# Softmax normalization moved ahead of a unit's last part, and a routing table's steps moved by one, in a fused decoder layer

## The chip, the cores and the metric

One Trainium2 chip, one of its NeuronCores. The metric is the device time of one execution in microseconds (us), as the median of several runs. The engines are named as the profile names them: PE (TensorE matmuls), PEld (TensorE weight loads), DVE (VectorE), ACT (ScalarE), POOL (GpSimd), SP (SyncE, which issues most of the DMAs). Each engine works through its own instructions in order; between engines there are semaphores.

## The reference, cut to what matters

One pre-norm decoder layer for 16 batches of 128 tokens with 256 channels, all in float32:

```python
x = x + attn(layernorm(x))          # 16 heads; keys and values are one shared latent of 72
x = x + birwkv(layernorm(x), ctx, ctx, w, u)   # two decaying scans over the tokens
x = x + moe(layernorm(x))           # 8 experts, top 2, hidden 512

# attn, for each head h
Wdkv = x @ latent_w + latent_b
q = x @ Wd_w[h] + Wd_b[h]
scores = q @ Wdkv.T / sqrt(d_head), masked causally
p = softmax(scores)                 # exp(s - max), then divided by its sum
y[h] = p @ Wdkv
out = concat(y) @ out_w + out_b
```

The expert part sends each token to two of eight experts. The kernel therefore makes lists of tokens for each expert and, from the counts, tables of "slots": one slot is 128 tokens of one expert.

## The kernel before

**Units and steps.** The attention is cut into units: one batch and 4 of its 16 heads, so 64 units (`NU`), 4 to a batch. A loop over steps `s` writes all instructions in a fixed order (`manual_schedule`: no scheduler reorders them). Step s holds the scores of unit s (L442, PE), their negated row maxima (`maxima`, L459, DVE), their exponentials with row sums (`exps`, L467, ACT, four activations), a mask for the unit after next (L454, ACT), then the query projections of the next group of two batches (`query_tile`, L404 on PE, evacuated by L410 on ACT), and, for unit s-2, the transposes of its probabilities (`turn_probs`, L486 on PE, L488 `aT` on ACT), their product with the values (`values`, L494 `py`) and its evacuation (L506, L509).

Between them lies the **normalization** of a unit: the reciprocal of the four sums (L479, DVE) and the product of the 128x512 exponentials with it, in place (L480, POOL). In the kernel before, unit s-1 is normalized near the start of step s, and its transposes follow in step s+1.

**The plan.** All other work is put into a step by a table: `at(step, place, fn, ...)`, with the places "pre", "A", "B", "C" and "D" in the order in which `run(s, place)` is called in a step. "C" is the last part of a step in the attention stage; there is little in "D" before step 64. What lies in "C" and uses DVE or POOL:

- `wkv_exps` of batch b in step 4b+1: ACT exponentials (L533, L535), then two POOL products (L536, L537). The scan L545 on DVE in the next step reads L536's output.
- for a group of batches that begins at step z (8, 16, ... 48): `group_stats` in step z-3 (L305, L306 on DVE, L300 on POOL), `group_norm` in step z-2 (L320 on DVE, then ACT), `group_latents_out` in step z (L374 `kvT` on DVE, which frees a PSUM bank that the logits `pl`, L652, then use).
- parts of `route`, the choice of experts: for batches 0 to 3 in steps 25 to 27, for 4 to 7 in 41 to 43, for 8 to 11 in 57 to 59. The second part (L684 to L689, steps 25, 41 and 57) and the fifth (L726 to L737, steps 27, 43 and 59) lie in "C". They are small DVE instructions. Part four begins with the matmuls `pf` (L705 to L708) in step 27, 43 and 59, in a PSUM bank that a query projection used before.
- the parts of `first_table(0)`, which after 8 batches fixes the first 9 slots: six parts in six steps. Part 1 is a matmul `pc` (L758) in a PSUM bank of the query projections and five small DVE instructions (L760 to L770), part 2 is L830 to L834, part 3 is L776 to L784, part 4 is L792 and L794, part 5 is L801 to L807, part 6 is L809 to L815. Then `list_slots` (step 52, "C") reads the finished table into a register of SP (L842) and loads the first lists.

Two batches' tail stages share DVE and POOL with this: in step 4b+8 `residual` (L573, then L305, L306, L298, L300), in 4b+9 `mix_1` and `mix_2` (L602, L607, L608, then L609 on POOL), in 4b+10 `mix_stats`, in 4b+11 `mix_shift` (L320) and `mix_row` (L625, ACT), then the turn of the row for the logits (L640, L645) and the logits.

**After the attention.** From step 64 on each step takes one expert slot (`fetch`, `bring`, `turn`, `up`, `down`, L912 to L1026). This stage does not touch the lines of the change, but the last unit's normalization lies in step 64, behind `turn(0)`.

**PSUM.** The tag "t" has two banks, shared by all transposes (`pt`, `pxn`, `px`, `pw`, `pn`); "mm" has two, shared by `pq`, `pk`, `pl`, `pf` and `pc`.

```python
def normalize(b, hg):
    pr, sums = probs[b, hg], sums_of.pop((b, hg))
    rsum = small.tile([P, HG], F32, tag="rsum", name=f"rsum_{b}_{hg}")
    nc.vector.reciprocal(rsum, sums)
    nc.gpsimd.tensor_mul(pr, pr, rsum.unsqueeze(2).to_broadcast([P, HG, T]))
```

Of the kernel before, what the change touches and what calls it, by code (L numbers as in the profile page):

```python
# [22 lines left out]
C = 256  # L23
# [10 lines left out]
NHG = H // HG  # L34
NU = B * NHG
# [44 lines left out]
def decoder_kernel(  # L80
# [328 lines left out]
    def query_tile_out(g, i, pq, to):  # L409
        nc.scalar.activation(to, pq[:, :GT], AF.Identity, bias=bq_sb[:, i : i + 1], scale=0.25)  # L410
# [23 lines left out]
    def scores(b, hg):  # L434
        g, i = divmod(b, GB)
        n = b * NHG + hg
        ps = sbank(n)
        if n < 2:

            nc.tensor.matmul(ps, identb, maskb, start=True, stop=False)  # L440
        for j in range(HG):
            nc.tensor.matmul(  # L442
                ps[:, j, :],
                q[g, hg][0:L, j, ts(i, T)],
                kvT[g][:, ts(i, T)],
                start=False,
                stop=(j == HG - 1),
                skip_group_check=n >= 2,
            )
        pss[b, hg] = ps  # L450

    def lay_mask(n):

        nc.scalar.copy(sbank(n), maskb)  # L454

    def maxima(b, hg):
        ps = pss[b, hg]
        nm = small.tile([P, HG], F32, tag="nm", name=f"nm_{b}_{hg}")
        nc.vector.tensor_reduce(nm, ps, AX.X, ALU.max, negate=True)  # L459
        sums_of[b, hg] = nm  # L460
# [15 lines left out]
# [6 lines that stand above are left out]
    def turn_probs(b, hg):  # L482
        pt = bank("t", f"pt_{b}_{hg}").rearrange("p (j t) -> p j t", j=HG)
        pr = probs.pop((b, hg))
        for j in range(HG):
            nc.tensor.transpose(pt[:, j, :], pr[:, j, :], ident)  # L486
        aT = wk.tile([P, HG, T], F32, tag="aT", name=f"aT_{b}_{hg}")
        nc.scalar.copy(aT, pt)  # L488
        aTs[b, hg] = aT

    def values(b, hg):
        g, i = divmod(b, GB)
        py = bank("y", f"py_{b}_{hg}", bufs=1).rearrange("p (j t) -> p j t", j=HG)
        nc.tensor.matmul(  # L494
            py[:L], kvN[g][:, ts(i, L)], aTs.pop((b, hg)), start=True, stop=True
        )
        pys[b, hg] = py
# [426 lines left out]
    def bring(j):  # L924


        t, k = slots[j]
        to = []
        for n, (engine, copy) in enumerate(zip(experts, (nc.scalar.copy, nc.vector.tensor_copy))):
            into = experts[engine]  # L930
            if k % 4 == 0 or j in RARE:
                load_values(t, "ex", j, k, engine, E - 1, into)
            w = hpools[0].tile([P, WU0], F32, tag=f"w{n}", name=f"w{n}_{j}")
            copy(w, wall[:, bass.ds(into.pop(j), 1), n * WU0 : (n + 1) * WU0].rearrange("p o w -> p (o w)"))
            to.append(w)
        brought[j] = to

    def turn(j):
        xr = xrs.pop(j)
        pt = bank("t", f"pxr_{j}")  # L940
        for c in range(NC):
            nc.tensor.transpose(pt[:, ts(c, P)], xr[:, ts(c, P)], ident)  # L942
        xT = hpools[0].tile([P, NC, P], F32, tag="xT", name=f"xT_{j}")
        nc.vector.tensor_copy(xT, pt[:, : NC * P].rearrange("p (c t) -> p c t", c=NC))  # L944
        xTs[j] = xT
# [85 lines left out]
    def at(step, place, fn, *args):  # L1031
        plan.setdefault((step, place), []).append((fn, args))

    def run(step, place):
        for fn, args in plan.pop((step, place), []):
            fn(*args)
# [103 lines left out]
    for b in range(B):  # L1140
        s = NHG * b
        if b + 1 < B:
            at(s + 2, "pre", load_ctx, b + 1)
        at(s + 1, "C", wkv_exps, b)
        at(s + 2, "B", wkv_back, b)
        at(s + 3, "A", wkv_back_add, b)
        at(s + 4, "B", wkv_forth, b)
        at(s + 5, "A", wkv_forth_add, b)
        at(s + 5, "B", project, b, (0, 1))
        at(s + 6, "B", project, b, (2, 3))  # L1150
        at(s + 6, "C", rest_values, b)
        at(s + 7, "B", project, b, (4, 5))
        at(s + 7, "C" if b < B - 1 else "B", project, b, (6, 7, NP))
        for name, (step, place) in {B - 2: last_but_one, B - 1: last}.get(b, usual).items():
            at(s + step, place, stages[name], b)
        if b < E:
            for k in range(3):
                at(s + 11 + k, "C", load_expert, b, k)
        if b % RB == RB - 1:
            r = b // RB  # L1160
            parts = ((13, "B"), (13, "C"), (14, "B"), (15, "B"), (15, "C"))
            if b == B - 1:
                parts = ((12, "B"), (12, "D"), (13, "B"), (13, "D"), (14, "B"))
            for step, place in parts:
                at(s + step, place, route_part, r)
            for k in range(2 * RB):
                if b < B - 1:
                    at(s + 16 + k, "A", route_part, r)
                else:
                    at(s + 14 + (k + 1) // 3, "CDA"[(k + 2) % 3 if k > 1 else k], route_part, r)  # L1170
        if b + 1 in FIRST_B:
            i = FIRST_B.index(b + 1)
            parts = [(18 + k, "C") for k in range(6)]
            if i:
                parts = [(18, "C"), (20, "D"), (21, "B"), (21, "D"), (22, "D"), (23, "D")]
            for step, place in parts:
                at(s + step, place, table_part, i, first_table, i)
            for k in range(0, S1[i], 2):
                at(s + 24 + k // 2, "C", list_slots, min(2, S1[i] - k))
        if b == B - 1:  # L1180
            for k in range(7):
                at(s + 15 + k // 3, "ABD"[k % 3], table_part, "2", last_table)
            for k in range(0, S2, 4):
                at(s + 17 + k // 4, "C", list_slots, min(4, S2 - k))
            for k in range(4):
                at(s + 20 + k, "B", table_part, "3", very_last)
            for k in range(0, S3, 4):
                at(s + 24 + k // 4, "C", list_slots, min(4, S3 - k))
# [30 lines left out]
    def ahead(n, what):  # L1219
        if n < len(ORDER):  # L1220
            what(ORDER[n])
# [8 lines left out]
    for s in range(SLOT0 + len(ORDER) + 1):  # L1230
        j = s - SLOT0
        unit = divmod(s, NHG)
        past = divmod(s - 2, NHG)
        if s < NU:
            scores(*unit)
        if j == 0:

            st.close()
            hpools.append(ctx.enter_context(tc.tile_pool(name="hp", bufs=2)))
            turn(0)  # L1240
        if 1 <= s < NU + 1:
            normalize(*divmod(s - 1, NHG))
        run(s, "pre")
        if 2 <= s < NU + 2:
            turn_probs(*past)
        run(s, "A")
        if j == 0:
            bring(0)
        if s < NU:
            maxima(*unit)  # L1250
            exps(*unit)
            if s + 2 < NU:
                lay_mask(s + 2)
        g, i = divmod(s, UG)
        tiles = [(0, t) for t in late_tiles.get(s, [])]
        if g + 1 < NG:
            tiles += [(g + 1, t) for t in (TILES_1 if g == 0 else TILES)[i]]
        made = [(n, t, *query_tile(n, t)) for n, t in tiles[:2]]
        run(s, "B")
        if 2 <= s < NU + 2:  # L1260
            values(*past)
            values_out(*past)
        for n, t, pq, to in made:
            query_tile_out(n, t, pq, to)
        for n, t in tiles[2:]:
            query_tile_out(n, t, *query_tile(n, t))
        for n, t in tiles:
            if t == NP:
                rest_queries(n)
            if t == 5 and n:  # L1270
                odd_queries(n, 0)
            if t == 7:
                odd_queries(n, 1)
        if j >= 0:
            ahead(j + AHEAD, fetch)
            ahead(j + 1, bring)
            ahead(j, up)
        run(s, "C")
        if j >= 0:
            ahead(j + 1, turn)  # L1280
            if j >= 1:
                down(ORDER[j - 1])
        run(s, "D")
        if j == SF + S2 - SKIP:
            for r in RARE:
                if_used(r, whole_slot)
# [55 lines left out]
```

## Time and profile before

| | before |
|---|---|
| runs | 555.1, 555.19, 555.8 us; median 555.19 |
| profiled execution | 554.7 us, its span 553.0 us |
| granted PE clock, mean | 0.984 of full speed |
| PE busy, 25 to 320 us (attention) | 284.6 of 295 us |
| PE busy, 320 to 553 us (experts) | 211.5 of 233 us |
| ACT busy, 25 to 320 us | 251.4 us |
| DVE busy, 25 to 320 us | 217.6 us |
| POOL busy, 25 to 320 us | 198.8 us |

The profile is of one execution; the span runs from its first to its last instruction, and the time of the run is 1.7 us longer. In the timelines below a row is: start in us from the span's beginning, duration in us, engine, line of the kernel, operation, output<-inputs, shape, number of instructions, and in brackets the idle time of the engine just before it and who ended it. A wait for several semaphores is put down to the one that came last in the profile, which is not always the true one. The group rows of the page give busy us in all, mean ns of one, then the engine's idle us ahead of the group and what ended most of it.

### The profile page before, as it was taken

To read this page: it belongs to the slowest core of one execution; us is meant where nothing else is said; L and a number is where in the kernel's file an instruction comes from. 1 tells how busy PE (TensorE), PEld (TensorE's weight loads), DVE (VectorE), ACT (ScalarE), POOL (GpSimd) and SP (SyncE) were. 2 spreads that over 40 slices of the span, in tenths; PEclk is the share of its full clock that TensorE was granted. 3 is DMA by queue.
4 is the path that set the end of the run, shared out by engine and by line. 5 is a ranking of instruction groups with operands and counts; after the bars stand their busy time and mean duration, and the time that the engine had idled before them with its cause. 6 is when DMAs were issued, how large, how long until landed. Compare 5 with 4: busy or idle time off the path is not lost. (4 is left out here: it accounts for less than half of the span.)

```text
span 553.0 us, 10138 instructions
## 1 busy us (share of the span) xinstructions
PE 512.8 (93%) x3272; PEld 439.2 (79%) x3272; DVE 330.6 (60%) x831; ACT 329.3 (60%) x953; POOL 327.1 (59%) x379
## 2 busy tenths in 40 slices
PE   4889999999999999999998989999989999989990
PEld 3768787887777887877875679989979999989980
DVE  3354776687887678888769776555644533333330
ACT  1788998898797888888986873434313232313200
POOL 5356647564787774697646976454875454541532
PEclk9999999999999999999998999999989999999996
DMA  5432245364365545131121113232234232325321
GB/s 149 98 88 67 70 133 170 121 198 120 110 182 133 170 130 178 41 98 37 52 79 56 40 53 66 38 65 45 40 40 51 48 51 47 51 47 173 58 30 19
DMA packets 39662, 47.59 MB, mean 86 GB/s; under 512 B 14136, under 2 KB 31416, under 8 KB 39576
## 3 DMA queue, kind: packets, MB, share of 16 engines
q1 hardware_dynamic: 30106, 37.20, 23.0%
q0 software_dynamic: 7936, 9.51, 11.2%
q8 instruction: 28, 0.46, 0.3%
q10 hardware_dynamic: 1566, 0.21, 0.3%
q14 instruction: 26, 0.21, 0.2%
HBM read 28.22 MB, written 13.31 MB: 75 GB/s over the span
## 5 line engine op out<-in xcount | busy, mean ns | idle before, releaser
L467 ACT ACTIVATE pr<-s,nm 128x128 f32<-128x128 f32 x256 | 90.7, 370 | 9.7 <-DVE nm L459 9.5
L480 POOL TENSOR_TENSOR pr<-pr,rsum 128x512 f32<-128x512 f32 x64 | 75.7, 1183 | 33.5 <-DVE rsum L479 25.6
L990 ACT ACTIVATE sl<-s 128x512 f32<-128x512 f32 x36 | 21.5, 598 | 120.7 <-PE s L980 104.9
L1018 POOL DMA_INDIRECT acc<-y,en x28 | 47.5, 1697 | 60.4 <-DVE y L1013 29.8
L442 PEld LDWEIGHTS s<-kvT,q 72*128 72x128 f32 x512 | 65.7, 191 | 18.7 <-issue 12.6
L980 PEld LDWEIGHTS s<-xT,w 128*128 128x128 f32 x576 | 70.5, 195 | 9.4 <-issue 6.7
L980 PE MATMUL s<-xT,w 128*128 128x128 f32 x576 | 72.0, 279 | 5.4 <-DVE xT L944 2.3
L520 PE MATMUL po<-outw_sb,yP 128*128 128x256 f32 x288 | 74.4, 385 | 0.6 <-DMA yP<-yd 0.6
L442 PE MATMUL s<-kvT,q 72*128 72x128 f32 x512 | 70.5, 279 | 3.2 <-DMA q<-qr 2.2
L980 PE MATMUL pu<-xT,w 128*128 128x128 f32 x576 | 70.5, 276 | 0.0
L992 DVE TENSOR_TENSOR hT<-sl,pu 128x512 f32<-128x512 f32 x36 | 24.7, 687 | 74.1 <-PE pu L980 56.9
L1002 PE MATMUL pd<-wall,hT 128*128 x288 | 68.0, 379 | 0.0
L494 PE MATMUL py<-aT,kvN 128*72 128x512 f32 x128 | 66.4, 600 | 1.6 <-ACT aT L488 1.3
L980 PEld LDWEIGHTS pu<-xT,w 128*128 128x128 f32 x576 | 67.7, 193 | 0.0
L404 PE MATMUL pq<-xnT,wq_sb 128*128 128x256 f32 x256 | 65.3, 387 | 0.0
L520 PEld LDWEIGHTS po<-outw_sb,yP 128*128 128x128 f32 x288 | 54.0, 193 | 13.1 <-issue 5.2
L459 DVE TENSOR_REDUCE nm<-s 128x4 f32<-128x512 f32 x64 | 43.6, 682 | 30.5 <-PE s L442 30.5
L1002 PEld LDWEIGHTS pd<-wall,hT 128*128 128x128 f32 x288 | 52.0, 190 | 5.6
L467 ACT ACTIVATION_READ_ACCUMULATOR pr<-s,nm 128x1 f32 x256 | 53.0, 207 | 0.0
L488 ACT COPY aT<-pt 128x512 f32<-128x512 f32 x64 | 37.2, 581 | 26.0 <-PE pt L486 24.6
L404 PEld LDWEIGHTS pq<-xnT,wq_sb 128*128 128x128 f32 x256 | 46.2, 195 | 5.0 <-issue 0.2
L912 POOL DMA_INDIRECT xr<-xn,en x36 | 37.4, 1040 | 13.3 <-issue 7.6
(172 smaller groups left out, 877.8 us busy)
## 6 DMA issues: line engine op xcount, KB each, us to landing
wall<-in_wg_dram SPq DMA_DIRECT2D x8, 512.0 KB
wall<-in_wu_dram SPq DMA_DIRECT2D x8, 512.0 KB
wall<-in_wd_dram SPq DMA_DIRECT2D x8, 512.0 KB
q<-q SPq DMA_DIRECT2D x16, 224.0 KB
yP<-yB SPq DMA_DIRECT2D x32, 112.0 KB
cx<-in_cx_dram SPq DMA_DIRECT2D x16, 128.0 KB
acc<-x SPq DMA_DIRECT2D x16, 128.0 KB
xn<-row SPq DMA_DIRECT2D x16, 128.0 KB
```

The lines of the kernel that those rows point to most:

```text
L404: nc.tensor.matmul(pq[:, :GT], w[:, c, :], xnT[g][:, c, :], start=(c == 0), stop=(c == NC - 1))
L442: nc.tensor.matmul(ps[:, j, :], q[g, hg][0:L, j, ts(i, T)], kvT[g][:, ts(i, T)], start=False, stop=(j == HG - 1), skip_group_check=n >= 2,)
L459: nc.vector.tensor_reduce(nm, ps, AX.X, ALU.max, negate=True)
L467: nc.scalar.activation(pr[:, j, :], ps[:, j, :], AF.Exp, bias=nm[:, j : j + 1], accum_out=sums[:, j : j + 1],)
L480: nc.gpsimd.tensor_mul(pr, pr, rsum.unsqueeze(2).to_broadcast([P, HG, T]))
L488: nc.scalar.copy(aT, pt)
L494: nc.tensor.matmul(py[:L], kvN[g][:, ts(i, L)], aTs.pop((b, hg)), start=True, stop=True)
L520: nc.tensor.matmul(pos[b][:, :C], yP[b][:, i, :], outw_sb[:, i, :], start=(i == 0), stop=(i == NP))
L912: nc.gpsimd.indirect_dma_start(out=xr, out_offset=None, in_=xn2[0 : t["rows"], :], in_offset=bass.IndirectOffsetOnAxis(ap=entries[j][:, 0: ...
L980: nc.tensor.matmul(o[:, ts(f, P)], w[:, c * F + f * P : c * F + (f + 1) * P], xT[:, c, :], start=(c == 0), stop=(c == NC - 1),)
L1002: nc.tensor.matmul(pd[:, :C], hT[:, f, :], wall[:, bass.ds(e, 1), WD0 + f * C : WD0 + (f + 1) * C], start=(f == 0), stop=(f == NF - 1),)
L1018: nc.gpsimd.indirect_dma_start(out=acc if j < SF + S2 else out2, out_offset=bass.IndirectOffsetOnAxis(ap=en[:, 1:2], axis=0), in_=y, in_of ...
```

## The change

The normalization of unit s is written in step s itself, after "B" and the queries and before "C", instead of in step s+1 before "pre". And the six parts of the first table (`first_table(0)`) go from steps 46 to 51 to steps 47 to 52; the last of them is then in the step and place in which `list_slots` first reads the table.

```diff
@@ the first table's parts @@
         if b + 1 in FIRST_B:
             i = FIRST_B.index(b + 1)
-            parts = [(18 + k, "C") for k in range(6)]
+            parts = [(19 + k, "C") for k in range(6)]
             if i:
                 parts = [(18, "C"), (20, "D"), (21, "B"), (21, "D"), (22, "D"), (23, "D")]
@@ the loop over the steps @@
             st.close()
             hpools.append(ctx.enter_context(tc.tile_pool(name="hp", bufs=2)))
             turn(0)
-        if 1 <= s < NU + 1:
-            normalize(*divmod(s - 1, NHG))
         run(s, "pre")
         if 2 <= s < NU + 2:
             turn_probs(*past)
...
             ahead(j + AHEAD, fetch)
             ahead(j + 1, bring)
             ahead(j, up)
+        if s < NU:
+            normalize(*unit)
         run(s, "C")
         if j >= 0:
             ahead(j + 1, turn)
```

## The prediction

> **What bounds the kernel now.** I read the page first (span, busy shares, groups), then the waits of the TensorE matmul row (PE) inside the attention part, 25 to 330 us, then the timelines of single engines at the places where the change has something to move.
>
> ```profile
> span 553.0 us, 10138 instructions
> ...
> PE 512.8 (93%) x3272; PEld 439.2 (79%) x3272; DVE 330.6 (60%) x831; ACT 329.3 (60%) x953; POOL 327.1 (59%) x379
> ...
> L480 POOL TENSOR_TENSOR pr<-pr,rsum 128x512 f32<-128x512 f32 x64 | 75.7, 1183 | 33.5 <-DVE rsum L479 25.6
> ```
>
> PE is busy 93% of the span and sets the time. The 33.5 us that POOL sits idle ahead of the normalization cost nothing by themselves: the normalized tile is read only two steps later. What counts is when PE waits:
>
> ```profile
> PE pt L486 <- POOL pr L480: 2.3, 2, 1.5
> PE s L442 <- DMA q<-qr: 1.5, 1, 1.5
> PE pt L486 <- DVE m L684: 1.3, 2, 0.7
> PE py L494 <- ACT aT L488: 1.3, 2, 0.6
> PE pw L598 <- DVE xT L944: 1.0, 1, 1.0
> PE pc L758 <- ACT q L410: 1.0, 1, 1.0
> ...
> PE pf L705 <- ACT q L410: 0.4, 2, 0.2
> ```
>
> Columns: total us, times, longest. In the whole attention part PE waits for a normalization twice, 1.50 us at 295.34 and 0.76 us at 318.37. The two waits put down to DVE m L684 (137.79 and 215.05) are not for it: there the transposes need the PSUM bank that L608 of mix_2 reads until 137.64, and L608 keeps its place. So the most the first edit can give is 2.3 us, and the second edit 1.04 us (pc L758, at 238.97).
>
> **The change, part by part.** 64 reciprocals (L479, 0.17 us on DVE) and 64 products (L480, 1.04 us on POOL alone) stay the same instructions. The order of instructions on each engine shows what moves: on DVE and POOL they go ahead of the "C" work of their own step; ACT and SP keep their order; on PE only the two pc matmuls go from step 46 to step 47. No DMA is added or moved in SP's order. In steps without C work on DVE or POOL nothing changes, since the reciprocal waited for the step's exponentials ahead of the next maxima before, too.
>
> *1. Steps 4b+1 (16 of them):* POOL does the product ahead of L536 and L537 (0.73 us each). These come 1.04 us later, and so does the scan L545 that reads L536's output. At 99 to 104 us: product 100.2 to 101.24, L536 to 101.97, L537 to 102.7, scan from 102.7 instead of 101.51, ending near 103.95; the next maxima (104.08) wait for PE until 104.05 anyway. Cost 0; with that cover gone, about 0.5 us each. No PE wait hung on these products, so no gain.
>
> *2. Step z-3, z-2, z:* the statistics, L320 and the latents' L374 come after the reciprocal. Their exponentials have ended by then (170.62 against L374 at 171.18), so each loses 0.09 us. Cost 0 to 0.1 in all. In steps 0 and 1 the reciprocal waits up to 0.2 us for the exponentials, and PE needs xnT 1.4 us after it is ready. Cost 0.
>
> *3. Router parts in steps 25 and 41.* Here is the trouble. DVE and POOL at step 25:
>
> ```profile
> 137.77 0.19 DVE L686 TENSOR_TENSOR oh<-src,m 128x32 f32<-128x32 f32 x1
> 138.00 0.60 DVE L687 TENSOR_TENSOR oh<-oh,rev 128x32 f32<-128x32 f32 x1
> 138.63 0.19 DVE L688 TENSOR_REDUCE first<-oh 128x4 f32<-128x32 f32 x1
> 138.85 0.43 DVE L689 TENSOR_TENSOR oh<-oh,first 128x32 f32<-128x32 f32 x1
> 139.21 0.16 DVE L479 RECIPROCAL rsum<-sums 128x4 f32<-128x4 f32 x1
> ```
>
> ```profile
> 137.79 0.77 POOL L609 TENSOR_TENSOR x<-x,r 128x256 f32<-128x256 f32 x1 [4.14 <-DVE m L684]
> 138.51 0.73 POOL L536 TENSOR_TENSOR kv<-kv,cx 128x256 f32<-128x256 f32 x1
> ```
>
> L687 takes 0.60 us instead of 0.19 and ends at 138.60, as POOL's L609 does (138.56); L689 takes 0.43 and ends with L536. L688, a reduction of one input, is not held. The Trainium skill, "SBUF — State Buffer", section "Who interferes with whom", says the same as a rule that speaks against this change: a DVE instruction with two SBUF inputs and a GpSimd instruction that reads SBUF exclude each other, and whoever issues first holds the ports for the whole instruction. Moving the reciprocal ahead of C releases a 1.04 us POOL product exactly while C's small two-input instructions run; before, the reduction L459 followed, which is not held. Without the rule, by durations alone, part 3 costs 0.09 us per place; with it: the reciprocal moves L686 from 137.77 to 137.86, 0.07 behind L609's start, so L686 is held to 138.60; L687 is then held by the product (138.51 to 139.55) to 139.60; L689 by L536, now 139.55 to 140.28. The maxima L459 start at about 140.45 instead of 139.49: +0.96. If L686 still gets in, only L689 is held by the product: +0.3. I take +1.0, because at 254.50 the like instruction L794, 0.03 behind L609's start, was held (0.79 us). Who waits for the maxima:
>
> ```profile
> 140.20 0.37 ACT L467 ACTIVATE pr<-s,nm 128x128 f32<-128x128 f32 x1 [1.16 <-DVE nm L459]
> ```
>
> ```profile
> 143.41 0.41 PE L705 MATMUL pf<-sel,before 128*128 128x32 f32 x2 [0.21 <-ACT q L410]
> ```
>
> ACT was already idle for them, and from 140.20 to 143.36 it works without a gap down to the L410 that frees pf's PSUM bank, for which PE already waits. So the +1.0 goes to PE whole: 1.0 us at step 25 and 1.0 at step 41, where the trace repeats itself (0.67 and 0.21 us). **+2.0 us**, bounds +0.6 and +2.4.
>
> *4. Router part in step 57.* The product follows L609 directly, 292.9 to 293.9 instead of 294.21 to 295.28; the transposes could start near 293.95 instead of 295.34. But PE's next matmul pf needs L694, behind maxima that slip as in part 3 (293.63 to about 294.65), and then py needs aT, behind exponentials that slip with them (294.31 to about 295.35). What is left of 1.4 us is about 0.3. In step 59 the two-input L730 are held by the product, and the maxima of step 60 come about 0.6 later; ACT has 0.2 us of room ahead of the copy at 307.15, so PE loses 0.4. Together **0**, bounds -1.4 and +0.5. The 0.76 us at 318.37 stay: POOL itself is busy (L741, L912, L300) until that product.
>
> *5. First table one step down, step 46 to 47.* PE no longer waits 1.04 us for pc: in step 47 only one query tile is made and its bank is free. But the chain of five small DVE instructions behind pc (L760 to L770, 1.2 us) now stands ahead of xnT, the residual and its statistics in step 48, which before had PE's pace as their only limit (DVE idle 0.48 and 0.60 us there). This chain ends in
>
> ```profile
> 248.68 0.46 DVE L374 TENSOR_SCALAR kvT<-pk,latb_c_sb 72x256 f32<-72x256 f32 x1
> ```
>
> ```profile
> 249.53 0.51 PE L652 MATMUL pl<-rw_sb,x2T 128*128 128x8 f32 x4
> ```
>
> and pl starts only when L374 has freed its bank. pc ends near 242.8, L760 to L770 run to about 244.5 (L766 held by POOL's L557, as it was held to 0.42 us before), xnT to 245.3, the residual at 245.25 (before: 245.15). So L374 and pl stand where they stood: the 1.04 us are won and given back. **0**, bounds -1.0 (chain fits) and +1.0 (L768 and L769 held by the product too).
>
> *6. The other table parts, steps 48 to 52.* Part 2 has 0.83 us of DVE idle behind it: 0. Part 3 in step 49 delays the maxima by 0.9 (255.49), but py has just enough room (aT by 260.65, needed 260.83): 0. Part 4 is earlier. In step 51 the part ran before at 258.84 or 261.33, ahead of the exponentials' end; now the reciprocal waits for them (262.16) and L801 to L807 follow, L805 held by L557 (262.68 to 263.78), L807 by the product (263.72 to 264.77). The residual starts near 265.0 instead of 263.40, the exponentials of step 52 by 1.6 later, x2T at 266.8 (pl was at 266.91: 0.45 lost), and aT of step 53 at 270.5 to 271.1 where py started at 270.41. **+0.8 us**, bounds 0 and +1.6. In step 52 SP's table load waits for the last part in the same step; SP's next need is the store at 272.19: 0.
>
> *Sum:* 2.0 + 0 + 0 + 0.8 = +2.8 us. The profiled execution took 554.7 us, its span of 553.0 and 1.7 around it: 557.5. It lies 0.5 below the median of the runs, 555.19 (555.1 to 555.8), so the median after is 555.19 + 2.8 = **558.0 us**.
>
> **The rivals.**
> A. *The pc wait is won and the port costs little.* DVE slips between POOL's instructions and the chain of part 5 fits: -1.0 from pc, -1.0 of the 1.4 in step 57, +0.6 in the routers: -1.4, 553.8 us. For it: POOL records are rough, and L686 misses by only 0.07 us. Against it: L687, L689, L694 (0.88), L711 (0.87) and L697 (1.03) all ended with a POOL instruction. This is the one that ends on the other side; it decides from the point where L686 starts ahead of L609 and L770 ends before 243.9.
> B. *The moves cancel:* +0.6 in the routers, -0.6 elsewhere, 555.2 us. PE has slack enough almost everywhere that most of the 64 moves are invisible; that speaks for it.
> C. *More is held:* all upper bounds of parts 3 to 6 at once, 2.4 + 0.5 + 1.0 + 1.6 = +5.5, 560.7 us. It needs every collision lost.
>
> **How the numbers follow.** The forecast (+1.2 to +4.5) has 0.53, C 0.08, B 0.19, A 0.20. About 0.2%, 1.1 us, is what a measurement of this kernel can tell from no change. Slower by more: 0.61; within: 0.19; faster: 0.20. The likeliest case alone spans 556.4 to 559.7; the range for 8 in 10 takes in B and half of A below and part of C above: 554.1 to 560.1.
>
> **What would show it.** Right: maxima L459 of step 26 about 1 us later against the scores, L686 and L687 near 0.7 and 0.9 us, the wait of pf for q at 1.0 us or more twice; no pc wait in the list; pl still right behind L374 in step 48; py waiting for aT in step 53; the 1.50 us of pt gone, but a wait of pf or py a little later. Wrong: L686 to L689 at 0.19 us under the product, pf's wait still 0.2, or the expert part (from 320 us on) starting earlier than before.

## The result and the profile after

| | before | after |
|---|---|---|
| runs (five each, in turn) | 553.7 to 557.4 us, median 555.19 | 560.7 to 562.5 us, median 561.08 |
| ratio, 95% interval | 1 | 1.0112 (1.009 to 1.0134) |
| profiled execution | span 553.0 us, clock 0.984 | span 559.3 us, clock 0.982 |

The change costs 5.9 us. The prediction said slower by 2.8 us (558.0, range 554.1 to 560.1): the side is right, the size is half of what was measured, and the measured median lies 1 us above the range.

The page of the changed kernel, the lines that answer to those shown of before:

```profile
span 559.3 us, 10150 instructions
...
PE 514.6 (92%) x3272; PEld 439.0 (78%) x3272; DVE 336.0 (60%) x831; ACT 328.5 (59%) x953; POOL 324.8 (58%) x379
...
L480 POOL TENSOR_TENSOR pr<-pr,rsum 128x512 f32<-128x512 f32 x64 | 66.5, 1040 | 35.9 <-DVE rsum L479 24.8
```

The products are 9.2 us less busy (1040 ns in place of 1183; before, single ones took up to 1.95 us beside a scan on DVE). Other POOL instructions fall beside those scans now and take most of it back (L300 and L741 together +7.4 us), so that POOL is 2.3 us less busy in all. DVE is 5.4 us busier, with the same 831 instructions. Those 5.4 us are the first hint: DVE does no more work, it is held longer. The waits of PE in the attention part, columns as before (total us, times, longest):

```profile
PE py L494 <- ACT aT L488: 2.2, 3, 1.0
PE pf L705 <- ACT q L410: 2.2, 2, 1.1
PE px L640 <- DVE xnT L353: 1.7, 1, 1.7
...
PE pq L404 <- DVE src L664: 0.8, 1, 0.8
PE pf L705 <- DVE sel L694: 0.8, 1, 0.8
...
PE pt L486 <- POOL pr L480: 0.6, 1, 0.6
```

The pc wait of 1.04 us is gone and the waits for normalized probabilities fell from 2.3 to 0.6 us: both aims were met. In their place stand the two pf waits, grown from 0.21 to 1.1 us each, and a wait that was not there at all, px for xnT, 1.67 us in step 48.

How late PE is in the changed kernel, read from the start of the product py of each unit against the trace of before, gives the places: +0.9 us in step 27, +0.9 in step 43, -1.5 in step 47, **+3.8 in step 48**, +1.5 in step 53, +2.3 in step 60; small steps of -0.2 and +0.7 in between cancel. At the end of the attention part it is 7.6 us late; the expert part then gives 1.3 back, because before had a stretch of low clock there (at 406 us, below) and this execution had none.

**Step 25, as predicted.** DVE, then POOL, then PE two steps later (start us, us, engine, line, operation):

```profile
137.24 0.17 DVE L479 RECIPROCAL rsum<-sums 128x4 f32<-128x4 f32 x1
...
137.51 0.72 DVE L686 TENSOR_TENSOR oh<-src,m 128x32 f32<-128x32 f32 x1
138.27 0.97 DVE L687 TENSOR_TENSOR oh<-oh,rev 128x32 f32<-128x32 f32 x1
...
139.49 0.43 DVE L689 TENSOR_TENSOR oh<-oh,first 128x32 f32<-128x32 f32 x1
```

```profile
137.46 0.73 POOL L609 TENSOR_TENSOR x<-x,r 128x256 f32<-128x256 f32 x1 [4.56 <-DVE rsum L479]
138.15 1.04 POOL L480 TENSOR_TENSOR pr<-pr,rsum 128x512 f32<-128x512 f32 x1
139.14 0.73 POOL L536 TENSOR_TENSOR kv<-kv,cx 128x256 f32<-128x256 f32 x1
```

```profile
143.97 0.41 PE L705 MATMUL pf<-sel,before 128*128 128x32 f32 x2 [1.09 <-ACT q L410]
```

Each DVE instruction ends 0.04 to 0.05 us after a POOL one: L686 with L609, L687 with the product, L689 with L536. L686 starts 0.05 us behind L609's start, as the prediction said it would (0.07).

**Steps 47 and 48, not as predicted.** DVE first, then POOL, then PE:

```profile
244.67 0.22 DVE L768 CAST wi<-wf 128x8 int32<-128x8 f32 x1
244.92 2.76 DVE L769 TENSOR_SCALAR wi<-wi 128x8 int32<-128x8 int32 x1
247.71 0.17 DVE L770 CAST wf<-wi 128x8 f32<-128x8 int32 x1
247.79 0.68 DVE L353 COPY xnT<-pxn 128x512 f32<-128x512 f32 x1
```

```profile
244.43 1.06 POOL L741 DMA_INDIRECT lists<-entry,place  x1 [0.18 <-DVE cnt L760]
245.49 0.12 POOL L750 MEMSET pad<- 128x1 f32 x1
245.55 1.10 POOL L557 TENSOR_TENSOR S<-S,bw 128x508 f32<-128x508 f32 x1
246.60 1.04 POOL L480 TENSOR_TENSOR pr<-pr,rsum 128x512 f32<-128x512 f32 x1
```

```profile
248.62 0.41 PE L640 MATMUL px<-ident,row 128*128 128x128 f32 x2 [1.67 <-DVE xnT L353]
```

L769 shifts eight integers on each partition and took 0.17 us before. Now it begins in the middle of the indirect DMA of the router's lists and ends only with the product, 2.76 us later, through four POOL instructions that leave no gap (0.01 us at most). xnT, which PE needs for px, waits behind it on DVE. The same happens to part 5 of the table in step 51, through the same row of POOL instructions (265.41 to 268.62):

```profile
266.19 2.47 DVE L805 TENSOR_TENSOR at<-iotas,at 128x9 f32<-128x9 f32 x1
```

**The clock.** The windows of the changed kernel about step 48 (length, then busy us and instructions of PE, PEld, DVE, ACT and POOL, then the granted clock):

```profile
244.00:248.00 4.00, 2.95 (x21) 2.56 (x20) 3.74 (x7) 2.50 (x5) 3.46 (x5) 1.00 0.14 40
248.92:252.33 3.41, 3.41 (x11) 2.22 (x10) 3.04 (x9) 1.99 (x9) 1.86 (x4) 0.50 0.17 58
252.40:256.00 3.60, 3.60 (x26) 3.01 (x25) 2.24 (x8) 1.92 (x5) 3.18 (x4) 1.00 0.03 5
```

After the idle time PE works for 3.41 us at half its clock: 11 matmuls where the next 3.60 us hold 26. In the profile of before there are two such windows ahead of the closing part (296.8 and 406.0 us, behind waits of 1.50 and 2.14 us), here three (248.9, and two in a row from 303.5).

### The profile page after: what moved, and what is told of

Its sections match the earlier page's. It is cut to its first block, busy times and chain, and to the rows that moved or that the text cites. A ratio compares the mean times of both kernels' runs of the same rounds, so it can differ in the third digit from the quotient of the medians.

```text
span 559.3 us, 10150 instructions
## 1 busy us (share of the span) xinstructions
PE 514.6 (92%) x3272; PEld 439.0 (78%) x3272; DVE 336.0 (60%) x831; ACT 328.5 (59%) x953; POOL 324.8 (58%) x379
## 5 line engine op out<-in xcount | busy, mean ns | idle before, releaser
L480 POOL TENSOR_TENSOR pr<-pr,rsum 128x512 f32<-128x512 f32 x64 | 66.5, 1040 | 35.9 <-DVE rsum L479 24.8
L980 PEld LDWEIGHTS s<-xT,w 128*128 128x128 f32 x576 | 69.2, 192 | 9.7 <-issue 6.7
L980 PE MATMUL s<-xT,w 128*128 128x128 f32 x576 | 70.8, 276 | 5.3 <-DVE xT L944 2.3
```

Of the source, the lines that this page charges most:

```text
L980: nc.tensor.matmul(o[:, ts(f, P)], w[:, c * F + f * P : c * F + (f + 1) * P], xT[:, c, :], start=(c == 0), stop=(c == NC - 1),)
```

## The experiments

One theory and three rivals at first. **T**: the loss sits in small DVE instructions that POOL holds, above all L769, and in the half-clock windows behind the idle time that this makes. **R1**: the moved normalization costs it everywhere. **R2**: the table's place alone costs it. **R3**: the reciprocal's wait for the exponentials does. Two more, P and K, come with their experiments. Each comparison has its own runs of the kernel before, so ratios are compared, not times.

| kernel | ratio to before, 95% | median us (before beside it) |
|---|---|---|
| changed kernel, again | 1.0098 (1.0067 to 1.0128) | 561.8 (554.6) |
| normalization alone | 1.0099 (1.0070 to 1.0128) | 557.9 (552.6) |
| table alone | 0.9998 (0.9981 to 1.0014) | 552.9 (552.6) |
| reciprocal early, product late | 1.0059 (1.0041 to 1.0077) | 555.6 (552.6) |
| part 1 in PSUM | 1.0042 (1.0025 to 1.0058) | 555.3 (552.6) |
| router behind the maxima | 1.0047 (1.0027 to 1.0067) | 557.6 (554.6) |
| both repairs | 1.0005 (0.9988 to 1.0022) | 553.0 (552.8) |
| unit 47 late | 1.0073 (1.0051 to 1.0095) | 557.1 (552.8) |
| 7 idle matmuls, step 48 | 1.0118 (1.0083 to 1.0153) | 558.6 (552.8) |
| 28 idle matmuls, three places | 1.0175 (1.0147 to 1.0203) | 564.7 (554.6) |
| selected steps | 0.9939 (0.9919 to 0.9959) | 551.5 (554.6) |

**The two parts of the change alone.** First the normalization without the table's move:

```diff
-            parts = [(19 + k, "C") for k in range(6)]
+            parts = [(18 + k, "C") for k in range(6)]
```

> Only the normalization moves; the first table's six parts stay in steps 46 to 51. Theory T (the loss is made in two places: the one-input integer shift L769 of the table's part 1 is held in step 47/48 by three POOL instructions in a row, and a TensorE idle time of 1.7 us there is followed by a clock window of 3.41 us at half speed; the moved product alone costs 0.9 us in each of the steps 25 and 41 and up to 2 us about step 58): the pf waits of 1.1 us stay, the pc wait of 1.04 us is back, L769 takes 0.2 us, no half-clock window about 249 us; 557 to 559 us, +2 to +4. Rival R1 (the moved normalization costs it everywhere, the table's step is beside the point): 560 to 561 us, as in the changed kernel. Rival R2 (the table's place alone costs it): 555 to 556 us.

Measured: +0.99%, as much as the whole change. T's 557 to 559 us holds the 557.9, but only because before was 2.6 us faster in this set; by the ratio, +5.5 us, R1's number came out and T's +2 to +4 did not. The trace says that it is still T's mechanism, one step up: PE is late in a few steps (0.9 us in 27 and in 43, 1.6 in 48 and 49, 1.1 in 52) and not everywhere. The pc wait is back (1.09 us), and now the table's part 1 in step 46 runs into the product of unit 46, which the early reciprocal has let go (DVE, then POOL):

```profile
242.16 2.19 DVE L766 TENSOR_SCALAR wf<-cnt 128x8 f32<-128x8 f32 x1
244.39 0.65 DVE L768 CAST wi<-wf 128x8 int32<-128x8 f32 x1
```

```profile
242.61 1.03 POOL L480 TENSOR_TENSOR pr<-pr,rsum 128x512 f32<-128x512 f32 x1
243.60 1.40 POOL L343 TENSOR_TENSOR x<-x,outb_sb 128x256 f32<-128x256 f32 x2
```

L766 ends 0.03 us after the first L343 (244.32), L768 0.03 us after the second (245.00). L766 was let in between two POOL instructions that leave no gap. And "L769 takes 0.2 us" was right and missed the point: another instruction of the chain was held.

Then the table's move without the normalization:

```diff
-            parts = [(18 + k, "C") for k in range(6)]
+            parts = [(19 + k, "C") for k in range(6)]
```

> Only the first table's parts move one step down; the normalization stays where it was. Theory T: the reciprocal then stands behind part 1, so the product cannot follow L557 while L769 waits; L769 is held to the end of L557 only, about 1.7 us in place of 2.76. The pc wait (1.04 us) is gone, PE idles about 0.6 us for xnT in step 48, not enough for a clock window; 554.8 to 556 us, -0.4 to +0.8. R1: 554 to 555 us (the pc wait is won, nothing else happens). R2: 557.5 to 558.5 us, the idle time of 1.67 us and the half-clock window about 249 us as in the changed kernel.

Measured: no change (0.9998). The pc wait is gone, R2 falls. But the chain was not held at all, and not to the end of L557 as T had it:

```profile
243.53 1.06 POOL L741 DMA_INDIRECT lists<-entry,place  x1 [0.18 <-issue]
```

```profile
243.62 0.17 DVE L769 TENSOR_SCALAR wi<-wi 128x8 int32<-128x8 int32 x1
243.82 0.17 DVE L770 CAST wf<-wi 128x8 f32<-128x8 int32 x1
```

L770 ends 0.46 us after the indirect DMA's start and gets through; in the changed kernel L769 starts 0.49 us after it and does not. For the hold itself this run told nothing.

**Which instruction holds.** The reciprocal goes ahead of C, the product stays at the start of the next step:

```diff
+        if 1 <= s < NU + 1:
+            product(*divmod(s - 1, NHG))
         run(s, "pre")
...
         if s < NU:
-            normalize(*unit)
+            normalize(*unit)      # the reciprocal only
         run(s, "C")
```

> As the changed kernel, but only the reciprocal goes ahead of C; the POOL product stays at the start of the next step. Theory T (the product is what holds DVE's small instructions): in steps 25 and 41 L686 to L689 are as long as before and the pf waits are back at 0.2 us (-1.8); about step 58 the same (-0.6 to -2.3, by whether a half-clock window falls there); on POOL the order about step 47 does not change, so L769 still takes 2.8 us and the half-clock window about 249 us stays: 557.5 to 559 us. Rival R3 (not the product but the reciprocal's wait for the exponentials delays C): 560.5 to 561.5 us, pf waits at 1.1 us.

Measured: +0.59%, between the changed kernel and before. The pf waits are 0.79 us, neither 0.2 nor 1.1. In step 25 of this kernel (L692 and L693 are L686 and L687 of the others):

```profile
137.56 0.73 DVE L692 TENSOR_TENSOR oh<-src,m 128x32 f32<-128x32 f32 x1
138.33 0.66 DVE L693 TENSOR_TENSOR oh<-oh,rev 128x32 f32<-128x32 f32 x1
```

The reciprocal alone pushes the comparison behind L609's start, and that is 0.58 of the 0.89 us; the product's longer hold is the rest. T had put all of it on the product: wrong, while the prediction's own working (L686 held by L609) was right. L769 escaped here too (0.17 us), against the expectation. L805 did not: it is held 2.65 us in step 51 (L811 of this kernel), so there the reciprocal alone, which waits for the exponentials, is enough.

**The hold of L769.** Two repairs of the changed kernel. In the first, part 1 reads and writes its integers in its PSUM bank, so that none of its instructions has both ends in SBUF:

```diff
-        nc.vector.tensor_scalar_add(f, c, float(add))
-        i = rp.tile([P, E], I32, tag=f"wi{name}", name=f"wi{name}")
+        nc.vector.tensor_scalar_add(f, pc[:, 0:E], float(add))
+        i = pc[:, E : 2 * E].bitcast(I32)
```

> As the changed kernel, but part 1 of the first table reads and writes its integers in its own PSUM bank (L766 reads pc, L768 to L770 use eight more columns of that bank), so that none of the five instructions has both ends in SBUF. Theory T: each takes about 0.2 us beside POOL, xnT is copied at about 245 us in place of 247.8, PE does not idle 1.67 us in step 48 and no half-clock window follows at 249 us: 3.2 to 3.8 us less than the changed kernel, 557.3 to 557.9 us. Rival R2 (the chain's place ahead of xnT costs it, held or not): 560 to 561 us. If the idle time goes but the clock window stays, the clock is not tied to the idle time: about 559.4 us.

Measured: 1.0042, against 1.0098 to 1.0112 of the changed kernel: some 0.6%, 3 us and more. The shift (L776 here, then the conversion back, L777) is as short as ever, and PE does not idle for xnT in step 48:

```profile
245.60 0.17 DVE L776 TENSOR_SCALAR pc<-pc 128x8 int32<-128x8 int32 x1
245.81 0.17 DVE L777 CAST wf<-pc 128x8 f32<-128x8 int32 x1
```

Two things changed at once here: the operands, and the chain's start, which no longer waits for L760's copy. The indirect DMA starts at 245.28, so the shift begins 0.32 us into it, at a point where nothing was held in the other kernels either; L777 begins 0.53 us into it and gets through, where L769 was held at 0.49. That the loss hangs on the hold is shown; that it is PSUM that lifts it rests on L777 alone (0.53 to 0.58 us into the DMA in the three kernels built so).

In the second, unit 47 alone is normalized at its old place; all else is the changed kernel:

```diff
+        if s == 48:
+            normalize(*divmod(s - 1, NHG))
...
-        if s < NU:
+        if s < NU and s != 47:
             normalize(*unit)
```

> As the changed kernel, but unit 47 alone is normalized at its old place, behind part 1 of the table. L769 begins at the same point of the indirect DMA as in the changed kernel. Theory T (a held instruction is let in when POOL has a gap, and the early reciprocal takes that gap away by making the product ready behind L557): L769 takes 1.7 to 1.8 us, to the end of L557, PE idles 0.5 to 0.7 us at px in place of 1.67; 1 to 2 us under the changed kernel. Rival (the product has nothing to do with it; the DMA or L557 alone hold L769 for 2.76 us): no change. If the chain misses the DMA and takes 0.2 us an instruction, the run tells nothing of this.

Measured: L769 starts 0.49 us into the indirect DMA, exactly as in the changed kernel, and takes 1.77 us. DVE, then POOL:

```profile
246.45 1.77 DVE L769 TENSOR_SCALAR wi<-wi 128x8 int32<-128x8 int32 x1
```

```profile
247.09 1.10 POOL L557 TENSOR_TENSOR S<-S,bw 128x508 f32<-128x508 f32 x1
248.65 1.04 POOL L480 TENSOR_TENSOR pr<-pr,rsum 128x512 f32<-128x512 f32 x1 [0.47 <-DVE rsum L479]
```

It ends with L557 (248.19), because the product now waits for a reciprocal that stands behind L769, and POOL has a gap. PE idles 0.73 us at px instead of 1.67. That is T's number, and the rival's is 2.76. The ratio, 1.0073, lies below the changed kernel's, though the intervals overlap.

**The router's parts.** In the changed kernel part 2 goes behind the next maxima:

```diff
-            parts = ((13, "B"), (13, "C"), (14, "B"), (15, "B"), (15, "C"))
+            parts = ((13, "B"), (14, "B"), (14, "B"), (15, "B"), (15, "C"))
```

> As the changed kernel, but the router's part 2 (L684 to L689) goes from C of its step to B of the next one, behind the row maxima. Theory P (as predicted: the held L686, L687 and L689 stand ahead of the maxima, and the pf wait follows): the maxima of steps 26, 42 and 58 come at once, the pf waits of 1.1 us in steps 27 and 43 are back near 0.2, and about step 58 some 0.6 to 2 us are won: 2.4 to 3.8 us under the changed kernel. Rival: the parts are held as long wherever they stand, and sel comes late for pf: under 0.5 us less than the changed kernel.

Measured: 1.0047, about 0.5% or 3 us under the changed kernel in the same set, inside theory P's 2.4 to 3.8 (the two intervals just touch). The pf waits on L410 are gone from the list. L686 is still held, even longer, but the maxima stand ahead of it:

```profile
136.71 0.68 DVE L459 TENSOR_REDUCE nm<-s 128x4 f32<-128x512 f32 x1
...
137.52 0.92 DVE L686 TENSOR_TENSOR oh<-src,m 128x32 f32<-128x32 f32 x1
```

A held instruction costs nothing where nobody waits behind it. In this kernel px still idles 1.66 us, with L769 held 2.76 us.

Both repairs at once:

> As the changed kernel, with both repairs at once: part 1 of the first table keeps its integers in its PSUM bank, and the router's part 2 stands behind the maxima of the next step. Theory T (the loss sits in these held DVE instructions, and the two places are independent): the repairs add up, -0.55% and -0.5%, so that the time comes within 0.2% of the kernel before, 0.998 to 1.002 of it. Rival (both repairs only remove the same clock windows, or the loss moves on to the next wait): 1.004 or more.

Measured: 1.0005, the time of before. The two repairs take the loss away, within 0.2%, and they add up. The gains of the change (pc, pt) are then in balance with what is left of its costs (L805 in step 51 stays).

**The clock windows.** First, useless matmuls where PE idles:

```diff
+    def filler(n, name):
+        w = bank("y", f"fill{name}", bufs=1)
+        for _ in range(n):
+            nc.tensor.matmul(w[:, :T], ident, ident, start=True, stop=True)
...
+    plan[48, "A"].insert(0, (filler, (14, "48")))    # and 6 in step 59, 8 in step 60
```

> As the changed kernel, with 28 matmuls of no use (128x128, 0.11 us apart) on PE where it only waits: 14 ahead of px in step 48, 6 ahead of pf in step 59, 8 ahead of py in step 60; they write a bank that py writes afterwards, and nothing reads them. Theory K (an idle time of about 1 to 1.7 us inside one clock window brings a half-clock window of 3.41 us, worth up to 1.7 us where PE is the bound): no half-clock window near 249 and 303 us, mean granted clock higher by about 0.005, 1.5 to 3.5 us under the changed kernel. Rival K0 (the windows fall by chance): the clock as in the changed kernel, the time the same or up to 0.5 us more.

Measured: 1.0175, slower than the changed kernel by 0.8%. The experiment was badly made: each matmul runs as two passes, so that 14 filled 3.1 us and not 1.55, and in step 59 the filler's bank is freed by an ACT copy that comes late:

```profile
PE fill L646 <- ACT yP L506: 3.5, 1, 3.5
```

That new wait of 3.5 us is followed by three half-clock windows in a row (302.4 to 312.7 us). It speaks for theory K (idle time brings the half-clock window), but not in the way that was meant. Made again with half the number, in step 48 alone:

> As the changed kernel, with 7 matmuls of no use (14 passes, 0.11 us apart, 1.55 us) on PE ahead of px in step 48, where it idles 1.67 us; they write a bank that py writes afterwards. L769 stays held for 2.8 us, and everything else as it was. Theory K (the idle time brings the half-clock window behind it): no half-clock window about 250 us, 0.3 to 1.5 us under the changed kernel, 1.007 to 1.0095 of the kernel before. K0 (the windows fall by chance): 1.0098 or a little more, a window about 250 us as often as without.

Measured: 1.0118 (1.0083 to 1.0153): no gain can be seen. Its one trace has no window about 250 us and no idle time there, so K is not refuted; the saving of at most 1 us is less than this comparison can tell. Inconclusive.

What told more were further traces of the changed kernel itself, which runs between 555.7 and 563.7 us at clocks of 0.970 to 0.989:

> The changed kernel once more, on the chip of the runs beside it, as the mark to compare them with. If the half-clock windows of 3.41 us are a chance of each execution, its profile has them at other places than 249 and 303 us; if they follow from the idle times of PE, at the same. L769 again takes over 2 us if its hold is a property of the order (theory T), 0.2 us if the 0.03 us by which the chain missed the indirect DMA decided it. 0.9 to 1.3% above the kernel before.

> The changed kernel, one more look (the same for the three beside it), to set its time, its half-clock windows and the length of L769 side by side in one execution each. If the slower ones have more half-clock windows and L769 held alike, the spread of 555.7 to 563.7 us is the clock's; if the fast ones have L769 at 0.2 us, it is the hold that comes and goes. By the traces so far: L769 held 2.76 us in each, windows between 0 and 6, about 1.2 us a window.

> As the look before it: L769 2.76 us, between 0 and 6 half-clock windows, each behind a stretch of 3.41 us with 0.7 us or more of PE idle time.

> As the look before it: L769 2.76 us, between 0 and 6 half-clock windows, each behind a stretch of 3.41 us with 0.7 us or more of PE idle time.

> As the look before it: L769 2.76 us, between 0 and 6 half-clock windows, each behind a stretch of 3.41 us with 0.7 us or more of PE idle time.

Measured: spans of 560.1, 557.2, 559.9, 560.2 and 559.1 us. With the first profile these are six traced executions. L769 takes 2.76 or 2.77 us and L805 2.46 or 2.47 in **all six**: the hold is a property of the order and no accident. The windows come and go, but only at a handful of places, each behind an idle time. One or two in a row fall about steps 57 to 60 in all six, one at 412 to 415 us in two; the others:

| place | PE idle | executions with a window | step costs PE without / with it |
|---|---|---|---|
| pf, step 27 | 1.1 us | 3 of 6 | 0.89 / 2.58 us |
| pf, step 43 | 1.1 us | 2 of 6 | 0.89 / 2.57 us |
| px, step 48 | 1.67 us | 3 of 6 | 2.80 / 3.81 us |
| pq, step 53 | 0.82 us | 1 of 6 | 1.47 / 3.05 us |

Step 27 in two of these executions, the same wait, with a window (first) and without (second):

```profile
145.10 0.41 PE L705 MATMUL pf<-sel,before 128*128 128x32 f32 x2 [1.09 <-ACT q L410]
...
147.19 1.70 PE L494 MATMUL py<-aT,kvN 128*72 128x512 f32 x2
148.68 2.52 PE L520 MATMUL po<-outw_sb,yP 128*128 128x256 f32 x6
```

```profile
144.65 0.41 PE L705 MATMUL pf<-sel,before 128*128 128x32 f32 x2 [1.10 <-ACT q L410]
...
146.73 1.02 PE L494 MATMUL py<-aT,kvN 128*72 128x512 f32 x2
147.59 1.46 PE L520 MATMUL po<-outw_sb,yP 128*128 128x256 f32 x6
```

The same eight matmuls take 1.7 us more. So an idle time of 1.1 us costs 1.1 us, or 2.8.

Which of the two goes with where the idle time lies against the clock's changes. These all fall on a grid of 3.41 us in a trace, and the grid lies differently in each execution. The 1.1 us of pf in step 27 was followed by half the clock in all seven traces in which it lay whole in one stretch of the grid, and in none of the four in which a bound divided it. The 1.67 us of px lay whole in one stretch in seven traces: half the clock followed in the three where it began 1.25 us or later in its stretch, and in none of the four where it began at 0.3 to 0.9 us. In step 43 the two with a window began at 0.6 and 1.25 us, and of the nine without it none lay whole and began before 1.29. This is read from kept traces; no run moved the grid.

**A version made from this.** The kernel before, with the normalization early only where it won without a collision, part 1 in PSUM and one step down, and the third router behind the maxima:

```diff
+    EARLY = (13, 21, 29, 37, 45, 57)
...
-        if 1 <= s < NU + 1:
+        if 1 <= s < NU + 1 and s - 1 not in EARLY:
             normalize(*divmod(s - 1, NHG))
...
+        if s in EARLY:
+            normalize(*unit)
         run(s, "C")
```

> A version made from the findings: the kernel before, with the normalization early only in steps 13, 21, 29, 37, 45 and 57 (in the first five the trace shows 0.2 us won each; in 57 the pt wait of 1.5 us), the third router's part 2 behind the maxima of step 58, the first table's parts one step down with part 1's integers in its PSUM bank. Theory T: -1.0 from pc, -1.0 from the five steps, -1.0 to -1.5 from step 57, and one half-clock window less about 297 us: 549 to 551.5 us where the kernel before has 552.6. Rival: won and given back further down, as most of the changed kernel's gains were: 552 to 553.5 us.

Measured: 0.9939, -0.61% or 3.4 us against the before of its set. The expected times were written for a before of 552.6 us; by the difference, -1 to -3.6 us, theory T's number came out. It is faster than both kernels. By its trace (span 550.1 us, clock 0.991) -0.2 us came in each of the steps 15, 23, 31 and 39, -1.5 in step 47, and no half-clock window fell ahead of the closing part.

## Why the prediction was wrong in size

The side and the mechanism were right: PE bounds the kernel, the early product holds DVE's small instructions, and most of the 64 moves are invisible. Term by term against before, with what each place costs where no half-clock window falls behind it (at steps 57 to 60, which have a window in all six traces, with the four that have one there, as before has):

| part of the prediction | predicted | measured |
|---|---|---|
| 1, 2: 4b+1 and group steps | 0 to +0.1 | -0.3 (-0.2 in some 4b+1 steps, some given back by DMAs of po) |
| 3: router, steps 25 and 41 | +2.0 | +1.8 |
| 4: router, steps 57 and 59, to the end of attention | 0 | about +0.6 |
| 5: first table, part 1 | 0 (-1.0 to +1.0) | **-1.5 + 2.8 = +1.3** |
| 6: other parts, step 51 above all | +0.8 (0 to +1.6) | +1.5 |
| half-clock windows | not in the sum | **about +1** |

*Part 3* held to a tenth at each place: L686 held by L609, L687 by the product, L689 by L536, the wait handed through ACT to pf. The third experiment even confirmed its split.

*Part 5 is the step that failed.* It had the wait removed from pc right (more than that came back, 1.5 us), and named L768 and L769 as candidates "held by the product too", at +1.0 as its far end. But it ran the chain "to about 244.5", with a single hold of 0.4 us, and so xnT to 245.3; xnT ended at 248.48. The row that it took this hold from was misread: it was put to L557, but in the kernel before L766 ran inside the indirect DMA and came out at the end of that (DVE, then POOL):

```profile
239.60 0.42 DVE L766 TENSOR_SCALAR wf<-cnt 128x8 f32<-128x8 f32 x1
```

```profile
238.99 1.06 POOL L741 DMA_INDIRECT lists<-entry,place  x1 [0.17 <-issue]
```

Besides, two things were missed. The hold need not end with one POOL instruction: L769 stayed out through L741, L750, L557 and L480 in a row. And the early reciprocal is what makes the row unbroken: with unit 47 normalized late, POOL has a gap behind L557 and L769 ends there (1.77 us). In those steps the trace of before showed no hold above 1 us, and so the range was built on single holds. But two rows elsewhere in it showed the longer kind and were not followed up. One is L834, behind the attention part; it was held through an indirect DMA (from 327.03 us) and the two POOL instructions after it, to 329.34:

```profile
327.40 1.97 DVE L834 TENSOR_TENSOR took<-sc 128x7 f32<-128x7 f32 x1
```

The other is of another batch (DVE, then POOL):

```profile
163.47 1.68 DVE L320 SCALAR_TENSOR_TENSOR nb_c<-mvc,rs_c 128x1 f32<-128x1 f32 x1 [1.18 <-POOL rs_c L300]
```

```profile
163.41 1.03 POOL L480 TENSOR_TENSOR pr<-pr,rsum 128x512 f32<-128x512 f32 x1
164.41 1.41 POOL L343 TENSOR_TENSOR x<-x,outb_sb 128x256 f32<-128x256 f32 x2
```

L320 starts 0.06 us behind the product and ends at 165.15: not with the product (164.44) but with the first of the two L343 that follow it (165.13). It got in ahead of the second, though POOL left no gap there; so did L686 between L609 and the product in step 25, and L687 between the product and L536. So a row of POOL instructions is the far end of what a hold costs and not its rule; what decides at which one DVE gets in stays open.

*Part 6* made the same error in smaller measure: L805 was to be held by L557 and L807 by the product; L805 was held through the indirect DMA and both (2.47 us). That the reciprocal's wait for the exponentials puts it there was right.

*Part 4* foresaw that the 1.50 us of pt would turn into waits of pf and py, and they did: 0.77 and 0.95 us in the first profile. The 0.76 us at 318.37 did not stay as they were; they are 0.6 to 1.1 in the six traces.

*The clock was left out altogether.* The sum treated an idle microsecond of PE as one microsecond. In the six traces a window behind it adds 1.0 to 1.7 us. The row of before that should have warned was there: the window at 296.8 us, right behind the 1.50 us wait that the change removed. The Trainium skill, "TensorE: Matmul & The Clock Gate", section "Part 1: The HAM clock gate", has in its table of the two states the rule of half the clock after at least one idle window, with free-running windows of about 3.4 us. The length agrees (3.41 us here), the condition does not: here the half-clock windows follow windows in which PE idled between 0.8 and 2.5 us of the 3.41 and worked the rest. By the rule as it stands the changed kernel would have had none in the attention part; the measurement decides. Where in its stretch the idle time lies goes with whether a window follows (above); what of PE's work counts in a stretch, and so why the bound is another at each place, remains open. The estimate of about +1 us is the median's 5.9 less the 4.9 of the table, not a measurement of its own.

*Rival C*, all collisions lost at 560.7 us, was the nearest number; it was given 0.08. Its mechanism is what happened in parts 5 and 6, and not in part 3.

## What to carry to other kernels

A small VectorE instruction with two inputs or both ends in SBUF is not safely priced at its duration, nor at the one GpSimd instruction beside it: the hold can last through the whole unbroken row of GpSimd work that it falls into (L769, four instructions, 2.76 us), though it often ends with the first (L687, 0.97 us). Look for what makes that row unbroken, for what stands behind the instruction in its queue, and put it behind the instruction that others wait for; PSUM operands may do as well, which rests here on one instruction. Where TensorE is the bound, a new wait of about a microsecond is priced at itself plus a share of a half-clock window (here 1.0 to 1.7 us, in one to three of six executions by the place). An early normalization that wins in six steps and loses in a few others is to be moved in those six: that kernel was the fastest here.

## What the runs showed of the hardware that was not expected

- An indirect DMA on POOL holds DVE's small SBUF instructions too, but not from the start of its row: L768 at 0.24 us, L770 at 0.29 us and the chains that ended by 0.46 us got through; L834, whose row starts at 0.37 us while the instruction before it runs to 0.45, and L769 at 0.49 us were held.
- Counted over the 17 traces in stretches of 3.41 us, laid so that the clock's changes fall on their bounds, from 17 us on to the closing part: of some 2,300 stretches at full clock with less than 0.7 us of PE idle time none was followed by half the clock; of 71 with 0.7 to 0.9 us, 6; of 76 with 0.9 to 1.2 us, 19; of 44 with 1.2 to 2 us, 7; of 5 with more, 5.
